# Layer 1 of a four-layer image network: narrower projection products, and the adding-up of the scan directions moved from VectorE to GpSimd

## The chip, the core and the metric

The kernel is one launch on one core of a Trainium2 chip. A core has five engines that run side by side, each with its own instruction queue that is worked off strictly in order: TensorE (PE, matrix products into the memory called PSUM), VectorE (DVE), ScalarE (ACT), GpSimd (POOL) and SyncE (SP, which here issues DMA transfers). Operands lie in SBUF (128 partitions) or in PSUM. The metric is the device time of the launch in microseconds, the median over several runs.

## The reference: what is computed

The input is 16 images of 96 channels and 56 x 56 pixels (L = 3136 pixels), in fp32. Layer 0 is a convolution block, layers 2 and 3 are spectral mixers with an 8-bit feed-forward part. The change is in layer 1 alone, a state-space block that scans each image in four directions (along the rows, along the columns, and both backwards):

```python
u = _ln(z, norm1_g, norm1_b) @ in_proj_w.T              # 96 -> 192 channels (Din)
uc = silu(depthwise_conv3x3(u))
xf = uc.reshape(B, Din, L)                               # pixels row by row
xt = jnp.transpose(uc, (0, 1, 3, 2)).reshape(B, Din, L)  # column by column
xs = jnp.stack([xf, xt, xf[..., ::-1], xt[..., ::-1]], axis=1)   # K = 4 directions
dbl = jnp.einsum('bkdl,kcd->bkcl', xs, x_proj_w)         # 8 rows for each direction
dts, Bs, Cs = jnp.split(dbl, [R, R + N], axis=2)         # R = 6, N = 1
dt = softplus(jnp.einsum('bkrl,kdr->bkdl', dts, dt_projs_w) + dt_projs_b[...])
a = jnp.exp(dt * A)
bb = dt * Bs * xs
# h[t] = a[t] * h[t-1] + bb[t], along L
y = h * Cs + Ds * xs
ym = sum of the four directions, each turned back to row order
z = z + _ln(ym, out_norm_g, out_norm_b) @ out_proj_w.T
z = z + gelu(_ln(z, norm2_g, norm2_b) @ fc1_w.T + fc1_b) @ fc2_w.T + fc2_b
return x + z
```

## The kernel before, in words

`kernel` (L1819) runs `layer0`, `layer1` and `layers23` one after the other. A second, general branch with `soft=True` is in the program too; it is entered only if a flag says so.

**Layer 1 (`layer1`, L839)** treats the 16 images one by one in four lanes that overlap: `fronts`, `makes`, `scans` and `backs` (L1398 to L1420). While one image is scanned, the front of a later image and the back of an earlier one run beside it.

- `front` (L998): squares and sums for the norm (L1028 to L1037), a reciprocal root on GpSimd (L1046), the projection to 192 channels (L1066), the 3 x 3 convolution as nine products of 64 x 64 tiles, four such tiles side by side (L1106), SiLU (L1129). Then `inputs` (L1136) makes the array `proj` of 128 x 3136: one product of all 128 columns for the four directions, 32 partitions for each (8 rows used, the others zero), in two parts of the contraction (L1142, L1143). ScalarE copies the upper half straight (L1145) and the lower half turned, into column order (L1150). A row of ones in `proj` (the bias `kone`) carries `dt_projs_b`. Four DMAs (L1159) write the B and C rows to a DRAM tensor `bc`.
- `made_of` (L1166): an image has 6 units in `ORDER` (`TILES`: 128 channels of direction 0, 1, 2 or 3, or the last 64 channels of two directions together), each in two halves, and each half in two subs of 784 pixels: 24 subs. For each, TensorE makes `p_d` (two products of 128 x 128 by 392 columns, L1183), ScalarE takes exp (L1190), ln(1 + .) (L1192), and exp of that times A (L1199). SyncE loads the B and C rows of the sub, repeated on all partitions, into a tile `bc` (L1210, L1214).
- `scanned` (L1221), on VectorE: for each sub `dt = dt * u` (L1254), `dt = dt * B` (L1257), the scan in place in `a` (L1261, backwards L1263), `dt = a * C` (L1269); then, for the first tile of an image accumulator, `y = u * D + dt` (L1274), and for all the others `y = y + dt` (L1280). Tiles 1 and 4 (`flip`) are in column order, so their L1254 and L1280 read `u` and `y` with a stride of 56 elements. At the end of an image one operation adds the turned half of `ym` (L1286).
- `back` (L1290): seven groups of 448 pixels, in two lanes (L1387): squares, output projection (L1309 to L1313), norms with two small reciprocal roots on GpSimd (L1328, L1351), transposes (L1357), the MLP (L1366 to L1376), the last sum (L1378) and the store (L1380).

**Order of the work.** Nothing is ordered by hand. Each step is announced by `yield Op(engine, cost, lag, take, give, ...)`, and `in_order` (L228) plays through all lanes with these costs and issues at each point the step that can start first; among equal starts the rank of its lane decides (L1400, L1405, L1411, L1417; less is earlier). So the costs and ranks fix each engine's queue when the program is built. `take` and `give` are counts of buffers (`buffers`, L846): "ps" are the PSUM pairs of two banks, "dt" the tiles of a sub.

Of the kernel before, what the change touches and what calls it, by code (L numbers as in the profile page):

```python
# [18 lines left out]
L = S * S  # L19
# [40 lines left out]
def packed(x):  # L60
# [32 lines left out]
    xp = np.zeros((P, 2 * P), f)  # L93
    wdt = np.zeros((P, 6, P), f)
    o["k_one"] = np.zeros((P, 1), f)
    for to, k in enumerate((0, 2, 1, 3)):
        xp[32 * to : 32 * to + R + 2, :DIN] = w("x_proj_w")[k]
        o["k_one"][32 * to + R + 2] = 1.0
        for i, halves in enumerate(TILES):
            at = 0  # L100
            for of, n in halves:
                if of == k:
                    d = slice(0, P) if n == P else slice(P, DIN)
                    wdt[32 * to : 32 * to + R, i, at : at + n] = w("dt_projs_w")[k, d].T
                    wdt[32 * to + R + 2, i, at : at + n] = w("dt_projs_b")[k, d]
                at += n
    o["l1_xp0"], o["l1_xp1"], o["l1_dt"] = xp[:, :P].T, xp[:, P:].T, wdt
# [731 lines left out]
def layer1(ctx, tc, src, given, dst, flags=None, soft=False):  # L839
# [3 lines left out]
    pairs, dram = ph.pool("ps", 4, space=PSUM), ph.pool("d", 3, space=bass.MemoryType.DRAM)  # L843
# [3 lines left out]
        "ps": 4, "x": 1, "half": 1, "xc": 2, "big": 7, "proj": 1, "dt": 5, "a": 2, "bc": 2, "xn": 1,  # L847
        "ysq": 1, "o": 2, "z": 2, "zn": 1, "zt": 1, "hid": 1, "xr": 2,
# [9 lines left out]
    n1, n2, no, xp0, xp1, wdt, kone, ds, fc1b, fc2, fc2b = ph.loads(  # L858
        "l1_n1", "l1_n2", "l1_no", "l1_xp0", "l1_xp1", "l1_dt", "k_one", "l1_d", "l1_fc1b", "l1_fc2", "l1_fc2b"
# [22 lines left out]
    def bounded():  # L882

        size = lambda out, in_: nc.vector.scalar_tensor_tensor(out, in_, -1.0, in_, ALU.mult, ALU.max)
        w, wx, wt = staged([C, DIN]), [staged([P, P]) for _ in range(2)], staged([P, 6 * P])
        nc.vector.tensor_tensor(w, win, win, ALU.mult)
        for out, in_ in (*zip(wx, (xp0, xp1)), (wt, wdt.rearrange("p i n -> p (i n)"))):
            size(out, in_)
        u, c, s = (ph.c([P, 2], n) for n in ("bound_u", "bound_c", "bound_s"))
        p = pair("p_b")  # L890
        for i, n in enumerate((P, 64)):
            nc.tensor.matmul(p[:n, 0, i : i + 1], w[:, P * i : P * i + n], ones[:C, 0, 0:1], start=True, stop=True)
        nc.vector.memset(u, 0.0)
        for i, n in enumerate((P, 64)):
            nc.vector.tensor_scalar(u[:n, i : i + 1], p[:n, 0, i : i + 1], float(C * C), None, ALU.mult)
# [102 lines left out]
    def front(b, it):  # L998
# [159 lines left out]
        for g in range(4):  # L1158
            nc.sync.dma_start(bc[g], proj[32 * g + 6 : 32 * g + 8])  # L1159
# [694 lines left out]
```

## Time and profile before

| quantity | us |
|---|---|
| median of 3 runs | 7367.89 (7360.73 to 7368.41) |
| the profiled execution, its own time | 7355.87 |
| its span, first to last instruction | 7354.1 |
| layer 1: first L1028 to last L1380 starts | 1163.7 to 4662.2 |
| last operation of an image's scan, L1286: first start, last start | 1459.8, 4505.3 |
| from there, one image of 15: (4505.3 - 1459.8) / 15 | 203.0 |

In the profile, "busy" is the time in which an engine executes; DMA-issuing, register and semaphore instructions are not counted. An fp32 product shows as two MATMUL records. "L1280" is line 1280 of the kernel before. In a group's row, the shapes are partitions x elements, output before input, then the count, busy time, mean of one, and after a bar the idle time of the engine just before these instructions with what ended it.

### The profile page before, as it was taken

How to read it: one execution, taken by the hardware profiler on the slowest of the kernel's cores; microseconds unless marked ns; L12 is line 12 of the kernel's file. 1: busy time of each engine (PE TensorE's matmuls, PEld its weight loads, DVE VectorE, ACT ScalarE, POOL GpSimd, SP SyncE). 2: the span in 40 equal slices, each digit the busy share in tenths (PEclk: the TensorE clock that was granted, in tenths of full speed). 3: DMA queues.
4: the chain of work that ended last, by engine and by line, in shares of the span. 5: the costliest groups of instructions: out<-in, count | busy, mean ns of one | idle time of the engine just before them, and what ended most of it. 6: DMA issues, size and time to landing. Idle time of an engine off the chain costs nothing. (4 is left out here: it accounts for less than half of the span.)

```text
span 7354.1 us, 114424 instructions
## 1 busy us (share of the span) xinstructions
PE 6443.1 (88%) x46263; PEld 4671.9 (64%) x46263; DVE 5719.1 (78%) x7601; ACT 4640.5 (63%) x6129; POOL 1011.2 (14%) x738
## 2 busy tenths in 40 slices
PE   7999997788999889888989887688999999999986
PEld 4444444455656666555666655587888888888875
DVE  6887792888889988888888986367777778777775
ACT  4544453677777777777777773256666666666664
POOL 0000000011111111111111112111111111111110
PEclk9999998899999999999999988799999999999997
DMA  1111111444444444344434432354555554555542
GB/s 38 29 39 39 32 32 34 134 116 126 121 120 128 121 118 124 113 116 115 116 115 124 121 109 66 88 118 101 125 123 130 114 126 111 122 130 123 122 109 59
DMA packets 494411, 743.59 MB, mean 101 GB/s; under 512 B 200065, under 2 KB 329633, under 8 KB 490434
## 3 DMA queue, kind: packets, MB, share of 16 engines
q1 hardware_dynamic: 492754, 732.54, 38.5%
q8 instruction: 367, 6.01, 0.4%
q0 software_dynamic: 1120, 3.64, 0.2%
q14 instruction: 170, 1.39, 0.1%
HBM read 544.06 MB, written 191.99 MB: 100 GB/s over the span
## 5 line engine op out<-in xcount | busy, mean ns | idle before, releaser
L1554 POOL TENSOR_TENSOR r<-v,nhalf 112x16 f32<-112x16 f32 (+1 forms) x128 | 396.8, 3106 | 2238.3 <-DVE v L1552 1681.7
L1183 PE MATMUL p_d<-proj,l_dt 128*128 128x392 f32 x1536 | 627.3, 536 | 40.5 <-ACT proj L1150 13.2
L1254 DVE TENSOR_TENSOR dt<-dt,big 128x784 f32<-128x784 f32 x384 | 457.3, 1191 | 122.0 <-ACT a L1199 121.8
L779 DVE SCALAR_TENSOR_TENSOR h<-pad,rows,h 128x1568 f32<-128x1568 f32 x288 | 525.8, 1844 | 3.9
L1190 ACT ACTIVATE dt<-p_d 128x784 f32<-128x784 f32 x384 | 315.2, 821 | 261.8 <-PE p_d L1183 252.0
L1183 PEld LDWEIGHTS p_d<-proj,l_dt 128*128 128x128 f32 x1536 | 289.7, 204 | 250.2 <-issue 88.2
L1612 PE MATMUL p<-k_f,z 112*128 112x112 f32 x3072 | 376.1, 282 | 61.5 <-DMA z<-d 57.5
L1375 PE MATMUL p_g<-l_fc,hid 128*112 128x96 f32 x2688 | 384.9, 281 | 47.4 <-ACT hid L1369 42.1
L1612 PEld LDWEIGHTS p<-k_f,z 112*128 112x128 f32 x3072 | 371.3, 199 | 70.4 <-issue 55.1
L1660 PE MATMUL p_v<-w,gg 128*112 128x97 f32 x2048 | 376.4, 266 | 36.7 <-DVE gg L1649 11.6
L1375 PEld LDWEIGHTS p_g<-l_fc,hid 128*112 128x112 f32 x2688 | 337.6, 193 | 96.7 <-ACT hid L1369 72.7
L1106 PE MATMUL p_c<-x,taps 64*64 64x392 f32 x4608 | 393.7, 491 | 1.1 <-ACT hid L1369 1.1
L1127 ACT COPY big<-p_c 64x392 f32<-64x392 f32 (+1 forms) x448 | 267.5, 598 | 197.8 <-PE p_c L1106 192.8
L1199 ACT ACTIVATE a<-dt,aneg 128x784 f32<-128x784 f32 x384 | 345.3, 936 | 64.7 <-DVE a L1263 55.0
L1328 POOL TENSOR_TENSOR r<-v,nhalf 112x4 f32<-112x4 f32 x112 | 226.7, 2024 | 1144.2 <-DVE v L1326 1144.2
L1269 DVE TENSOR_TENSOR dt<-a,bc 128x784 f32<-128x784 f32 x384 | 373.5, 973 | 9.0
L1257 DVE TENSOR_TENSOR dt<-dt,bc 128x784 f32<-128x784 f32 x384 | 373.6, 973 | 8.7
L1661 PE MATMUL p_v<-w2both,gg 128*112 128x97 f32 x2048 | 374.3, 265 | 0.0
L1192 ACT ACTIVATE dt<-dt,one 128x784 f32<-128x784 f32 x384 | 363.9, 948 | 8.9
L1261 DVE TENSOR_TENSOR_SCAN a<-a,dt 128x784 f32<-128x784 f32 x192 | 352.3, 1835 | 5.6
L1263 DVE TENSOR_TENSOR_SCAN a<-a,dt 128x784 f32<-128x784 f32 x192 | 352.0, 1833 | 4.1
L1581 PE MATMUL p_a<-first,xt 97*112 97x192 f32 x1792 | 336.2, 335 | 17.1 <-ACT xt L1575 6.9
(341 smaller groups left out, 16502.6 us busy)
## 6 DMA issues: line engine op xcount, KB each, us to landing
bc<-bc SPq DMA_DIRECT2D x256, 784.0 KB
bc<-bc SPq DMA_DIRECT2D x256, 392.0 KB
d<-y SPq DMA_DIRECT2D x448, 192.0 KB
z<-d SPq DMA_DIRECT2D x128, 672.0 KB
d<-uu SPq DMA_DIRECT2D x256, 169.8 KB
z<-d SPq DMA_DIRECT2D x192, 194.0 KB
xc<-x SPq DMA_DIRECT2D x96, 336.0 KB
x<-in_x SPq DMA_DIRECT2D x16, 1176.0 KB
```

Of the source, the lines that this page charges most:

```text
L779: nc.vector.scalar_tensor_tensor(out, view, taps9[:, i : i + 1], out, ALU.mult, ALU.add)
L1106: nc.tensor.matmul(p[to : to + 64, b, :TC], taps[64 * s : 64 * s + 64, j, k], pad[64 * s : 64 * s + 64, r0 : r0 + 7, k % 3 : k % 3 + S], s ...
L1183: nc.tensor.matmul(p[:, b, :TC], wdt[:, i], proj[:, cols], start=True, stop=True)
L1192: nc.scalar.activation(dt, dt, AF.Ln, bias=one)
L1254: nc.vector.tensor_tensor(as_own(dt), as_own(dt), own(u), ALU.mult)
L1257: nc.vector.tensor_tensor(dt, dt, t[:, 0], ALU.mult)
L1269: nc.vector.tensor_tensor(dt, a, t[:, 1], ALU.mult)
L1375: nc.tensor.matmul(p[:Q, q, :C], hid[:, j, own], fc2[:, j], start=j == 0, stop=False)
L1554: nc.gpsimd.tensor_tensor(r, v, nhalf[:, :n], ALU.pow)
L1612: nc.tensor.matmul(p[:, q, :Q], flat[:, P * (3 * q + k) : P * (3 * q + k) + P], f2, start=True, stop=True)
L1660: nc.tensor.matmul(out, gs[2 * h][:, at + k], w["w2"][:, 2 * h], start=True, stop=False)
L1661: nc.tensor.matmul(out, gs[1][:, at + k], w["w2both"][:, h], start=False, stop=True)
```

## The change

1. **Products of 32 columns.** In place of `inputs`, three products of 32 stationary columns for each chunk of 392 pixels: one for directions 0 and 2, one whose moving operand is `u` read across (column order), one for the remaining 64 channels of both. Chunks 0 to 3 go to the four groups of 32 output partitions of one PSUM bank, chunks 4 to 7 to those of the next. `proj` shrinks to 128 x 2 x 392: its partition says the chunk and the row, and one ScalarE copy fills it. All four directions' rows lie together (24 rows of dt input, 8 rows of B and C).
2. **Products of 32 rows.** `p_d` contracts over the 32 partitions of its chunk; the two halves of a sub lie on different groups of 32 partitions and in different banks. The bias `dt_projs_b` is added by ScalarE's activation.
3. **`bc`** is ordered by chunk; the loads move the same bytes into the same tiles.
4. **The scan's input lies in PSUM.** `dt * B` is written to a fixed PSUM tile `driven` of two banks, and the scan reads it there; the pool of PSUM pairs has three instead of four.
5. **GpSimd adds `y = y + dt`.** The 16 additions of an image that are not the first of their accumulator leave VectorE's list; a new lane `sums` issues them on GpSimd after the multiplication by C. `dt` is given back only after that. L1286 waits for the last of them.
6. **Plan.** Ranks of the four lanes, the number of `dt` (5 to 4), `proj`, `xn`, `o`, `z`, `xr` buffers, and three lanes in `back` instead of two.

```diff
-    pairs, dram = ph.pool("ps", 4, space=PSUM), ph.pool("d", 3, space=bass.MemoryType.DRAM)
+    pairs, dram = ph.pool("ps", 3, space=PSUM), ph.pool("d", 3, space=bass.MemoryType.DRAM)
+    driven = ph.pool("drive", 1, space=PSUM).tile([P, 2 * 512], F32, tag="drive", name="drive")
...
-        "ps": 4, "x": 1, "half": 1, "xc": 2, "big": 7, "proj": 1, "dt": 5, "a": 2, "bc": 2, "xn": 1,
-        "ysq": 1, "o": 2, "z": 2, "zn": 1, "zt": 1, "hid": 1, "xr": 2,
+        "ps": 3, "x": 1, "half": 1, "xc": 2, "big": 7, "proj": 2, "dt": 4, "a": 2, "bc": 2, "xn": 2,
+        "ysq": 1, "o": 3, "z": 3, "zn": 1, "zt": 1, "hid": 1, "xr": 3,
...
-        it["proj"] = proj = buf([P, L], "proj")
...
-                nc.tensor.matmul(p[:, b, :T], xp0, us[0][:, cols], start=True, stop=False)
-                nc.tensor.matmul(p[:, b, :T], xp1, us[1][:, cols], start=False, stop=True)
...
+        it["proj"] = proj = buf([P, 2, TC], "proj")
+        chunk = lambda t, c: t[:, TC * c : TC * c + TC]
+        across = lambda t, c: turned(t)[:, 7 * c : 7 * c + 7]
+        for b in range(2):
+            yield pe(3, 0.7, ("ps",) if b == 0 else ())
+            p = pair("p_x") if b == 0 else p
+            for k in range(3):
+                for q in range(4):
+                    moving = (chunk(us[0], 4 * b + q), across(us[0], 4 * b + q), chunk(us[1], 4 * b + q))[k]
+                    nc.tensor.matmul(p[32 * q : 32 * q + 32, b, :TC], xw[:, k], moving, start=k == 0, stop=k == 2)
+        yield act(2 * TC, give=("ps",))
+        nc.scalar.copy(proj, p[:, :, :TC])
+        it["bc"] = bc = dram.tile([8, 2, 4, TC], F32, tag="bc", name="bc")
         yield Op("SP", 1.4, 4.0, post=it["ready"])
...
+        for q in range(4):
+            nc.sync.dma_start(bc[:, :, q], proj[32 * q + 4 * R : 32 * q + 32])
...
-                    yield pe(2, 0.66)
+                    yield pe(1, 0.75)
                     p = pair("p_d")
                     for b in range(2):
-                        cols = slice(HALF * h + SUB * s + TC * b, HALF * h + SUB * s + TC * b + TC)
-                        nc.tensor.matmul(p[:, b, :TC], wdt[:, i], proj[:, cols], start=True, stop=True)
+                        on = slice(32 * (2 * s + b), 32 * (2 * s + b) + 32)
+                        nc.tensor.matmul(p[:, b, :TC], wdt[on, i], proj[on, h], start=True, stop=True)
...
-                        nc.scalar.activation(flat, p[:, :, :TC], AF.Exp)
+                        nc.scalar.activation(flat, p[:, :, :TC], AF.Exp, bias=dtb[:, i : i + 1])
...
-                    nc.vector.tensor_tensor(dt, dt, t[:, 0], ALU.mult)
+                    b = driven[:, :SUB]
+                    nc.vector.tensor_tensor(b, dt, t[:, 0], ALU.mult)
...
-                        nc.vector.tensor_tensor_scan(a, a, dt, first, ALU.mult, ALU.add)
+                        nc.vector.tensor_tensor_scan(a, a, b, first, ALU.mult, ALU.add)
...
-                    yield dve(SUB, give=("bc",) + (("a",) if end else ()))
+                    yield dve(SUB, give=("bc",) + (("a",) if end else ()), post=None if i in (0, 2) else added[unit, s])
                     nc.vector.tensor_tensor(dt, a, t[:, 1], ALU.mult)
...
-                        yield dve(SUB, 1.85e-3 if flip else 1.04e-3, give=give + (("big",) if free else ()))
-                        nc.vector.tensor_tensor(own(y), own(y), as_own(dt), ALU.add)
...
+            yield Op("none", 0.0, 0.0, wait=it["summed"])
             yield dve(L, 1.85e-3)
             nc.vector.tensor_tensor(image(ym[:64]), image(ym[:64]), turned(ym[64:]), ALU.add)
 
-        yield from scan()
+        def sums():
+            for unit in units:
+                i, h = unit
+                back = i >= 3
+                if i in (0, 2):
+                    continue
+                for s in ((1, 0) if back else (0, 1)):
+                    at = HALF * h + SUB * s
+                    yield Op("none", 0.0, 0.0, wait=added[unit, s])
+                    y, u = it["y"][i == 5], (um if i == 5 else u0)
+                    dt = made[unit][s]
+                    if i in (1, 4):
+                        out = turned(y)[:, at // S : at // S + 14]
+                        dt = dt.rearrange("p (w h) -> p w h", h=S)
+                    else:
+                        out = y[:, at : at + SUB]
+                    free = i in (4, 5) and unit == [k for k in units if k[0] == i][-1] and s == 0
+                    yield Op("POOL", 1.9, give=("dt",) + (("big",) if free else ()), post=it["summed"] if free and i == 5 else None)
+                    nc.gpsimd.tensor_tensor(out, out, dt, ALU.add)
+                    if free:
+                        big.append(u)
+
+        yield [scan(), sums()]
...
-        yield [some(range(0, NT, 2)), some(range(1, NT, 2))]
+        yield [some(range(k, NT, 3)) for k in range(3)]
...
-            yield 3 * b - 9
+            yield 3 * b + -3
             yield from front(b, items[b])
...
-            yield -1
+            yield -100
...
-            yield 99
+            yield -200
...
-            yield 3 * b
+            yield 3 * b + 3
```

## The prediction

> **What bounds the kernel now.** First the table by stages. The 13 images between 1663 and 4302 us each take 203.0 us, and the last back part runs alone from 4505 on (columns: start:end and length, then busy time and count of each engine, the granted clock, the DMA share, GB/s).
>
> ```profile
> core 0: us, PE busy (x) PEld busy (x) DVE busy (x) ACT busy (x) POOL busy (x), PEclk, DMA share, GB/s
> 1663.00:4302.00 2639.00, 2367.34 (x16488) 1579.00 (x16489) 2317.30 (x2693) 1967.85 (x2542) 450.62 (x378) 0.94 0.41 119
> 4505.00:4665.00 160.00, 116.58 (x761) 90.41 (x759) 45.92 (x115) 39.24 (x75) 33.17 (x35) 0.84 0.09 23
> ```
>
> Divided by 13, an image has PE 182.1 us busy, DVE 178.3, ACT 151.4, POOL 34.7. Two engines are near 90% of 203, and neither fills it: in fixed queues each waits some 20 to 25 us for the other. A change has to relieve both. Next, who makes DVE wait in that stretch (total, times, longest):
>
> ```profile
> DVE z L1378 <- PE p_g L1376: 108.1, 24, 9.9
> DVE dt L1254 <- ACT a L1199: 41.5, 42, 4.7
> DVE zn L1353 <- POOL r L1351: 36.6, 41, 1.2
> ```
>
> The largest wait is for PE (8.3 us an image). Then the groups by shape in the same stretch, which price what the change touches:
>
> ```profile
> L1183 PE MATMUL p_d<-proj,l_dt 128*128 128x392 f32 x1240 | 505.5, 534 | 18.4 <-ACT x L1070 12.4 <-ACT zt L1360 3.3 <-DVE z L1337 1.2
> L1254 DVE TENSOR_TENSOR dt<-dt,big 128x784 f32<-128x784 f32 x312 | 371.6, 1191 | 41.5 <-ACT a L1199 41.5
> L1106 PE MATMUL p_c<-x,taps 64*64 64x392 f32 x3744 | 320.3, 491 | 1.1 <-ACT hid L1369 1.1
> L1263 DVE TENSOR_TENSOR_SCAN a<-a,dt 128x784 f32<-128x784 f32 x156 | 285.9, 1833 | 3.1
> L1280 DVE TENSOR_TENSOR big<-big,dt 128x784 f32<-128x784 f32 x207 | 271.3, 1311 | 5.4
> L1106 PE MATMUL p_c<-half,taps 64*64 64x392 f32 x1872 | 160.1, 491 | 0.0
> L1142 PE MATMUL p_x<-big,l_xp 128*128 128x448 f32 x182 | 83.4, 539 | 0.0
> L1150 ACT ACTIVATE proj<-p_x,k_one 64x896 f32<-64x896 f32 x38 | 73.8, 1942 | 0.6
> ```
>
> Last, the question on which the result hangs: what do DVE and POOL do to each other? The timeline of two short POOL operations, each with the DVE operations beside it (start, duration):
>
> ```profile
> 2031.08 1.85 DVE L1261 TENSOR_TENSOR_SCAN a<-a,dt 128x784 f32<-128x784 f32 x1
> 2032.96 0.97 DVE L1269 TENSOR_TENSOR dt<-a,bc 128x784 f32<-128x784 f32 x1
> 2031.31 2.42 POOL L1328 TENSOR_TENSOR r<-v,nhalf 112x4 f32<-112x4 f32 x1 [11.98 <-DVE v L1326]
> ...
> 2885.24 0.17 DVE L1037 COPY me<-p_s 112x8 f32<-112x8 f32 x1 [0.63 <-PE p_s L1035]
> 2884.70 1.01 POOL L1328 TENSOR_TENSOR r<-v,nhalf 112x4 f32<-112x4 f32 x1 [15.94 <-DVE v L1326]
> ```
>
> Alone, the root takes 1.01 us. Beside a scan with two SBUF inputs it takes 2.42: it stands until the scan ends at 2032.93 and finishes 0.80 us later. It gets in at the 0.03 us between two DVE operations that depend on each other, before L1269.
>
> [...] The trace shows only the 64x64 case: L1106's 5616 records are 54 groups of four products per image, and (320.3 + 160.1) / 13 / 54 = 0.68 us for four, where one lone 128x128 product of L1183 takes 505.5 / 13 / 48 = 0.81 us.
>
> **Part by part, per image.**
>
> *L1280 leaves DVE:* 271.3 / 13 = 20.9 us, so 178.3 - 20.9 = 157.4. The product by B into PSUM and the scan from it: existing DVE rows with a PSUM operand (L1337, 548 ns) cost what those without do (L1335, 550 ns), so zero; bounds -0 and +0.05 us on 48 operations, 2.4 us.
>
> *Sixteen additions on POOL:* [...] 1.9 us[...]; 30 us in all. POOL's time is free (34.7 + 30 of 203). Half of them write and read `y` in column order; on DVE that stride makes 0.97 us into 1.66 (L1254's view by line: 960 ns least, 970 median, 1683 most), so the bound above is 1.9 x 1.7 = 3.2 us for those[...].
>
> *What they do to DVE* is the unknown. An addition is released when L1269 ends. DVE's next operation is mostly the next sub's L1254, two SBUF inputs, already started when POOL arrives; POOL waits. L1257 depends on L1254, so there is a gap, and by the timeline above POOL gets in there. L1257 has two SBUF inputs too and stands until the addition is over; behind it stand the scan, L1269, and every front and back step on DVE. The scan from PSUM[...] comes afterwards. Bounds: 0 (all adds fall under scans) and 16 x 1.9 = 30 us, more with the stride. I take 25: some adds meet one-input operations (L1337, L1344, L1346, L1378, together 15 us an image) or a DVE that waits anyway, at L1286 for one. DVE is then occupied for 157.4 + 25 = 182 us, slightly more than before.
>
> *PE:* four records of a sub's `p_d` take 1.48 us in the timeline; two products side by side (1.48 - 0.17) / 2 + 0.17 = 0.83, so 24 x 0.83 = 19.9 in place of 38.9. `p_x`: (83.4 + 83.2) / 13 = 12.8 become six groups of four, 6 x 0.83 = 5.0; if the reads across are twice as slow, 6.4; if columns don't run side by side, 16. PE falls to 155 (up to 166).
>
> *ACT:* the two copies into `proj`, (39.0 + 8.0 + 73.8 + 12.8) / 13 = 10.3, become one of 0.8: 142. [...]
>
> *SP and DMA:* as many loads of the same bytes; DVE never waits for `bc` in this stretch, so zero; the cover is the second tile, 8 us long. The four stores of B and C shrink in rows, zero.
>
> *Buffers:* three PSUM pairs for four, four `dt` for five, and `dt` held 2 to 4 us longer by POOL. These give waits back: more lanes against fewer pairs. Roots on POOL can stand behind an addition, 1.9 us, 14 times, in three lanes.
>
> *Sum.* DVE's idle 24.7 us shrinks, as PE, its main releaser, has 27 us less; the scans now also rank first. I put 11 us (bounds 8 and 17). 182 + 11 = 193 per image, 10 less than 203; over 15 images -150. The last back part: seven groups in two lanes are four rounds of 40 us in 160; in three lanes three rounds, 120, but PE alone needs 117, so 135: -25. The first front, with its `p_x` and copies on the only path: -8. Together -183 from the profiled execution's 7355.9 (span 7354.1 and 1.8 around it): 7173. The shown median, 7367.9, lies 12 above; on its scale 7185, and I say 7180.
>
> **Rivals.** *(A) The additions ride under the scans for nothing.* For it: 1.9 us of adding against 1.83 us of scan, and a PSUM operand was chosen; POOL may be refused at the gap. Against it: roots do get in at such gaps. DVE 160, PE 155: idle as now, 17; 177 per image: 15 x -26 - 33 = -423, so 6945. *(B) Slower: each addition holds DVE longer than the 1.31 us it saves, by too much.* DVE stands for t per addition: 157.4 + 16 t - 5 hidden + 13 idle = 205 is break-even with the 33 us of tail and front counted, so t = 2.5 us. With 3.2 us for the strided half the mean is 2.5; with contention on both, or a slower addition, 2.8: 210 per image, 15 x 7 - 33 = +72, so 7440. *(C) The narrow products don't run side by side*, as the trace shows only 64x64: PE stays at 182 + 3, DVE at 182, both bounds remain: 202 per image, 7330.
>
> **How the numbers follow.** Forecast case 0.50 (idle 8 to 17 and hold 20 to 30 us: 7080 to 7300), A 0.22 (6890 to 7060), C 0.06, B 0.22, of which 0.03 ends within 0.2%. 0.2% is 15 us, about what a measurement of this kernel tells from no change. Faster 0.77, same 0.03, slower 0.20. The likeliest case's own range is 7080 to 7300; the range for 8 in 10 takes in most of A and the near part of B: 6920 to 7420.
>
> **What would show it.** Right: POOL additions of about 1.9 us alone and near 3 when they wait; L1257's successor with idle time or a duration near 2.7 us behind such an addition; DVE's busy time near 157 or, if the stand is counted as busy, 182; PE near 155, `p_d` halved; ACT 142. A would show additions starting or stretching into scans with DVE's L1257 at 0.97 us and no gap. B would show them at 2.5 us or more with DVE standing as long. Wrong altogether: DVE idle for ACT's `a` or for PSUM pairs by more than 20 us an image, which would put the bound in the buffers.

## The result, and the profile after

| | before | after |
|---|---|---|
| median of 4 runs each, us | 7365.27 (7360.73 to 7368.41) | 7282.26 (7275.73 to 7297.03) |
| ratio, 95% interval | | 0.9891 (0.9873 to 0.9908) |
| the profiled execution / its span | 7355.87 / 7354.1 | 7277.09 / 7275.2 |
| granted TensorE clock, mean over the span | 0.934 | 0.906 |
| last operation of a scan (L1286; after: L1270), first start | 1459.75 | 1450.04 |
| the same, last start | 4505.26 | 4475.40 |
| from there to the last store of layer 1 | 157.0 | 109.0 |

The change gains 83 us, 1.1%. The forecast was 7180, a gain of some 185: the direction and the range hold, the size does not. The rows split the profiled gain of 78.8 us: the first image -9.7 (forecast -8), the 15 scans -20.1 (forecast -150), the tail -48.0 (forecast -25). So the missing gain is in the scans, which fall short by 130 us; the tail gave 23 us more than was forecast and makes up for a part of it.

The stages of after, ten images in steady state and the tail (columns as in the table by stages of before):

```profile
core 0: us, PE busy (x) PEld busy (x) DVE busy (x) ACT busy (x) POOL busy (x), PEclk, DMA share, GB/s
2066.40:4079.80 2013.40, 1772.14 (x13154) 1129.74 (x13153) 1835.93 (x1954) 1472.17 (x1926) 787.98 (x462) 0.89 0.42 121
4475.50:4584.50 109.00, 96.11 (x705) 78.93 (x703) 40.16 (x101) 34.48 (x67) 21.34 (x25) 0.94 0.10 26
```

Divide the first line by ten: a period of 201.3 us, DVE 183.6 busy, PE 177.2, ACT 147.2, POOL 78.8. The forecast had 193, 182, 155 and 142. DVE is as occupied as was said; its idle time is 17.7 us where 11 was put, and PE is busy for hardly less than before's 182.1. ACT's 147.2 holds 2.2 us that the forecast did not count: the exp that carries the bias takes 0.915 us in the median (L1180 of after), the exp without it 0.823 (L1190 of before), 24 times an image. The clock in this stretch is 0.89, where before had 0.94. The second line is the tail: PE is busy for 96 us of it and not for the 117 of before, at a clock of 0.94 and not 0.84.

What VectorE waits for in the same ten images (total, times, longest):

```profile
DVE dt L1243 <- ACT a L1189: 55.6, 42, 2.1
DVE z L1384 <- PE p_g L1382: 49.5, 32, 2.9
DVE me L1037 <- PE p_s L1035: 12.5, 27, 0.8
DVE zn L1359 <- POOL r L1357: 12.3, 10, 1.5
DVE v L1331 <- ACT o L1323: 5.7, 10, 1.5
DVE xn L1061 <- PE p_r L1056: 5.2, 11, 0.8
```

Beside the three waits that the prediction shows, before has these in its 13 images:

```profile
DVE me L1037 <- PE p_s L1035: 33.5, 38, 1.7
DVE v L1325 <- ACT o L1317: 32.3, 15, 2.9
DVE xn L1061 <- PE p_r L1056: 9.2, 7, 3.1
```

The 8.3 us an image for `p_g` have become 5.0, and the wait for ACT's `a` has grown from 3.2 to 5.6. All the waits of DVE that the profile puts down to PE add up to 11.7 us an image before and to 6.8 after, those for ACT to 5.8 and 6.3. The long waits for `p_g` have gone (longest 2.9 us, before 9.9). The groups by shape of the same ten images:

```profile
L1290 POOL TENSOR_TENSOR big<-big,dt 128x784 f32<-128x784 f32 x160 | 431.8, 2699 | 564.8 <-DVE dt L1259 414.2 <-PE p_f L1372 54.7 <-DMA x<-z 41.5
L1247 DVE TENSOR_TENSOR drive<-dt,bc 128x784 f32<-128x784 f32 x240 | 394.1, 1642 | 5.1
L1243 DVE TENSOR_TENSOR dt<-dt,big 128x784 f32<-128x784 f32 x240 | 307.2, 1280 | 58.2 <-ACT a L1189 55.6 <-POOL big L1290 2.4
L1173 PE MATMUL p_d<-proj,l_dt 32*128 32x392 f32 x960 | 245.9, 590 | 116.9 <-DVE z L1343 49.0 <-DVE z L1384 44.2 <-ACT hid L1375 11.1
L1253 DVE TENSOR_TENSOR_SCAN a<-a,drive 128x784 f32<-128x784 f32 x120 | 219.5, 1829 | 2.9
L1143 PE MATMUL p_x<-big,l_xw 128*32 128x392 f32 x480 | 69.1, 723 | 0.0
```

The counterpart of L1247 in before's 13 images, and all additions of after (count, then shortest, median and longest in ns):

```profile
L1257 DVE TENSOR_TENSOR dt<-dt,bc 128x784 f32<-128x784 f32 x311 | 302.6, 973 | 6.9
L1290 POOL TENSOR_TENSOR big<-big,dt x256: 1837/2451/4027, 1319.0 to 4473.3; 128x784 f32<-128x784 f32 x128
```

An addition takes 2.70 us on POOL in the mean of the ten images. Of the 256, the 128 that write `y` in column order take 2.23 us at the least, the other 128 take 1.84. The product by B (L1247) takes 1.64 us in the mean, where L1257 took 0.97: it has no new idle time in front of it, so its standing still is counted as busy. The scan from PSUM, 1.83 us, costs what it cost from SBUF.

How this happens shows in the timeline around one addition (start, duration):

```profile
2545.89 0.97 DVE L1259 TENSOR_TENSOR dt<-a,bc 128x784 f32<-128x784 f32 x1
2546.78 1.63 DVE L1243 TENSOR_TENSOR dt<-dt,big 128x784 f32<-128x784 f32 x1
2548.45 2.90 DVE L1247 TENSOR_TENSOR drive<-dt,bc 128x784 f32<-128x784 f32 x1
2551.38 1.85 DVE L1253 TENSOR_TENSOR_SCAN a<-a,drive 128x784 f32<-128x784 f32 x1
...
2547.03 3.48 POOL L1290 TENSOR_TENSOR big<-big,dt 128x784 f32<-128x784 f32 x1 [3.84 <-DVE dt L1259]
```

The addition is issued at 2547.03, stands behind L1243, which ends at 2548.41, gets in at the gap of 0.04 us, and ends at 2550.51. L1247 begins at 2548.45, ends at 2551.35, 0.84 us after the addition, and so lasts 2.90 us in place of 0.97. That is the picture that the prediction drew from the small operations on POOL (the reciprocal roots).

### The profile page after: what moved, and what is told of

It reads as the page before. It is cut to its first block, busy times and chain, and to the rows that moved or that the text cites. A ratio compares the mean times of both kernels' runs of the same rounds, so it can differ in the third digit from the quotient of the medians.

```text
span 7275.2 us, 115240 instructions
## 1 busy us (share of the span) xinstructions
PE 6324.3 (87%) x46587; PEld 4522.3 (62%) x46587; DVE 5752.0 (79%) x7344; ACT 4529.8 (62%) x6019; POOL 1682.2 (23%) x994
## 5 line engine op out<-in xcount | busy, mean ns | idle before, releaser
L1290 POOL TENSOR_TENSOR big<-big,dt 128x784 f32<-128x784 f32 x256 | 691.0, 2699 | 957.4 <-DVE dt L1259 756.8
L1247 DVE TENSOR_TENSOR drive<-dt,bc 128x784 f32<-128x784 f32 x384 | 627.5, 1634 | 12.8 <-DMA bc<-bc 4.5
L1243 DVE TENSOR_TENSOR dt<-dt,big 128x784 f32<-128x784 f32 x384 | 489.7, 1275 | 162.4 <-ACT a L1189 159.6
L1173 PE MATMUL p_d<-proj,l_dt 32*128 32x392 f32 x1536 | 404.9, 613 | 171.4 <-DVE z L1343 58.8
L1180 ACT ACTIVATE dt<-p_d,l_dtb 128x784 f32<-128x784 f32 x384 | 350.9, 914 | 275.1 <-PE p_d L1173 226.4
L1381 PE MATMUL p_g<-l_fc,hid 128*112 128x96 f32 x2688 | 393.3, 289 | 24.8 <-ACT hid L1375 10.8
L1253 DVE TENSOR_TENSOR_SCAN a<-a,drive 128x784 f32<-128x784 f32 x192 | 351.3, 1830 | 4.8
L1251 DVE TENSOR_TENSOR_SCAN a<-a,drive 128x784 f32<-128x784 f32 x192 | 351.1, 1829 | 4.1
L750 PE MATMUL p_c<-pad,taps 64*64 64x392 f32 x4032 | 347.3, 493 | 0.3 <-ACT pad L732 0.3
## 6 DMA issues: line engine op xcount, KB each, us to landing
d<-y SPq DMA_DIRECT2D x448, 192.0 KB
```

The source lines that it names most:

```text
L1173: nc.tensor.matmul(p[:, b, :TC], wdt[on, i], proj[on, h], start=True, stop=True)
L1243: nc.vector.tensor_tensor(as_own(dt), as_own(dt), own(u), ALU.mult)
L1247: nc.vector.tensor_tensor(b, dt, t[:, 0], ALU.mult)
L1290: nc.gpsimd.tensor_tensor(out, out, dt, ALU.add)
L1381: nc.tensor.matmul(p[:Q, q, :C], hid[:, j, own], fc2[:, j], start=j == 0, stop=False)
```

## The experiments

**The theories.** The forecast theory: a POOL addition holds DVE for about 1.56 us (25 us for 16), and the rest is DVE's idle time, which TensorE's lighter work shrinks. Once the result was known, three explanations stood for the idle time that did not shrink: the buffers (three PSUM pairs, four `dt`), the order in which the plan lays out the steps, and the lower clock. A rival to all: the additions cost much more than they hold DVE for.

"Same order" below means that every engine's queue has the order of the kernel named; "anew" that costs or buffers in the plan changed, so that the order was laid out anew. The image is the mean of nine images in steady state, busy times are per image with overlaps counted once, both from each run's own profile. (Before's first five images are shorter, so its 206.2 here stands beside 203.0 over all fifteen.) The ratio is to runs of the kernel before made beside it (medians 7351 to 7365).

| run | order | median us | ratio to before (95%) | image | PE | DVE | clock |
|---|---|---|---|---|---|---|---|
| before | | 7365 | 1 | 206.2 | 184.9 | 180.2 | 0.95 |
| after | | 7282 | 0.9891 (0.9873 to 0.9908) | 201.4 | 177.6 | 183.5 | 0.89 |
| no_adds | after's | 7059 | 0.9607 (0.9590 to 0.9624) | 185.8 | 169.7 | 158.9 | 0.94 |
| adds_dve_same | after's | 7178 | 0.9757 (0.9740 to 0.9773) | 195.3 | 174.4 | 177.5 | 0.91 |
| pd_twice | after's | 7413 | 1.0082 (1.0065 to 1.0099) | 210.0 | 191.9 | 182.2 | 0.91 |
| adds_dve | anew | 7343 | 0.9986 (0.9977 to 0.9995) | 209.0 | 176.0 | 178.5 | 0.88 |
| late_c | anew | 7297 | 0.9926 (0.9908 to 0.9944) | 205.3 | 181.1 | 168.0 | 0.89 |
| narrow_only | anew | 7177 | 0.9764 (0.9746 to 0.9782) | 191.1 | 171.9 | 178.2 | 0.94 |
| n_jitter | anew | 7308 | 0.9937 (0.9917 to 0.9956) | 197.5 | 173.4 | 178.5 | 0.91 |
| n_pairs3 | anew | 7651 | 1.0399 (1.0381 to 1.0416) | 228.9 | 191.2 | 180.7 | 0.84 |
| n_ranks | anew | 7481 | 1.0176 (1.0159 to 1.0193) | 216.5 | 185.3 | 178.5 | 0.86 |
| n_lanes3 | anew | 7457 | 1.0138 (1.0121 to 1.0155) | 215.7 | 181.4 | 180.0 | 0.85 |
| after_pairs4 | anew | 7429 | 1.0103 (1.0087 to 1.0120) | 219.8 | 189.6 | 179.3 | 0.86 |
| narrow_same | before's | 7463 | 1.0147 (1.0130 to 1.0164) | 212.8 | 182.0 | 180.1 | 0.86 |
| same_wide1 | before's | 7476 | 1.0171 (1.0154 to 1.0188) | 214.4 | 192.0 | 180.6 | 0.91 |
| same_narrow2 | before's | 7569 | 1.0296 (1.0279 to 1.0313) | 219.9 | 198.5 | 180.6 | 0.88 |
| same_wide2 | before's | 7551 | 1.0272 (1.0255 to 1.0289) | 220.6 | 202.8 | 180.6 | 0.95 |

**1. no_adds: after without the additions.**

```diff
-                    nc.gpsimd.tensor_tensor(out, out, dt, ALU.add)
```

> The changed kernel with its 16 GpSimd additions an image left out (12 of 24 subs of two accumulators then lack their sum; the plan and every queue stay as they are). Theory 'hold': the additions cost VectorE 26 us an image (39.4 + 30.7 - 23.3 - 28.6 and the small operations that stood, about 24 us by the groups), so VectorE falls from 183.6 to about 159 us and the image from 201.5 to 180 to 185: 7282 - 15 x 19 = about 7000 us. Rival 'PE and plan': TensorE, its lower clock and the fixed order with three PSUM pairs bound the image at 201; then the time stays within 7230 to 7290 us although VectorE's busy time falls.

Measured: 7059, an image of 185.8 us. The nine images of after and of no_adds, and the product by B in no_adds:

```profile
2267.50:4079.70 1812.20, 1598.26 (x11863) 1017.73 (x11863) 1651.06 (x1755) 1322.19 (x1729) 714.66 (x414) 0.89 0.42 121
2222.70:3895.20 1672.50, 1527.14 (x11864) 998.72 (x11862) 1429.75 (x1755) 1316.67 (x1729) 321.16 (x270) 0.94 0.45 131
L1247 DVE TENSOR_TENSOR drive<-dt,bc 128x784 f32<-128x784 f32 x216 | 211.8, 981 | 4.6
```

The durations of DVE's operations add up to 167.4 us an image here and to 192.2 in after, in the same order: the 16 additions hold DVE for 24.8 us, 1.55 each; 16.0 of it is the product by B, 2.1 the product by `u`, and the rest small operations of the front and the back. The period differs by 15.6 us only, since 26.9 us of idle (185.8 - 158.9) have become 17.9: a third of the hold falls where DVE waited anyway. The idle time matters as much: with no additions at all, DVE has 27 us to wait. The forecast's rival A had put 177 for this case.

**2. adds_dve_same: the additions on VectorE, in after's order.**

```diff
-                    nc.gpsimd.tensor_tensor(out, out, dt, ALU.add)
+                    nc.vector.tensor_tensor(out, out, dt, ALU.add)
```

> The changed kernel with its own plan to the letter: each of the 16 additions an image is issued at the same place of the order, but on VectorE instead of GpSimd. Theory 'hold': VectorE gets 20.9 us an image of additions (1.31 us each) in place of 24.8 us of standing, so the image is about as long as the changed kernel's or 2 to 3 us shorter: 7230 to 7285 us. If moving them to GpSimd did relieve VectorE: longer than 7320 us.

```profile
2239.40:3997.40 1758.00, 1569.90 (x11864) 1009.97 (x11864) 1597.77 (x1899) 1321.47 (x1729) 334.76 (x270) 0.91 0.43 125
```

7178, 104 us less than after, 195.3 us an image against 201.4. The only difference is the engine of the addition. On DVE the 16 take 20.9 us, on POOL they hold DVE for 24.8. With overlaps counted once, DVE is busy for 177.5 us and in after for 183.5, and its idle time is alike, 17.8 and 17.9: so the 6.1 us an image that the move costs are DVE's own busy time. Part 5 of the change, taken by itself in this order, is a loss, and what gains lies in the other parts.

**3. narrow_only and adds_dve: the parts separately, order laid out anew.** narrow_only is before with parts 1 to 3 alone (and two `proj` tiles). adds_dve is after with the additions issued on VectorE by the plan, right behind the product by C.

```diff
-                    yield pe(2, 0.66)
+                    yield pe(1, 0.75)
-                        cols = slice(HALF * h + SUB * s + TC * b, HALF * h + SUB * s + TC * b + TC)
-                        nc.tensor.matmul(p[:, b, :TC], wdt[:, i], proj[:, cols], start=True, stop=True)
+                        on = slice(32 * (2 * s + b), 32 * (2 * s + b) + 32)
+                        nc.tensor.matmul(p[:, b, :TC], wdt[on, i], proj[on, h], start=True, stop=True)
```

> The kernel before with the narrow products alone (32-column and 32-row products, bias in the activation, new order of bc); scan from SBUF, four pairs, five dt, additions on VectorE, ranks and two lanes as before. Theory 'PE term': TensorE's work falls by some 20 us an image by the groups' rows, VectorE's stays at 178; the image goes from 203 to about 195, the time to about 7250 us. Rival 'clock': [...] the granted clock falls from 0.95 towards 0.89 and gives most of TensorE's saving back, the image stays at 200 to 203, 7320 to 7365 us.

> The changed kernel with the 16 additions back on VectorE (narrow products, scan from PSUM, three pairs, four dt, ranks and three lanes kept; the plan is laid out anew). Theory 'hold': an addition on GpSimd costs VectorE as much (about 24 us an image) as the addition itself did (20.9 us), so the time is the same or a little better than the changed kernel's: 7220 to 7290 us. Rival 'GpSimd relieves VectorE': the image gets about 10 to 20 us longer, 7400 us and more.

narrow_only gives 7177 and an image of 191.1 us, without the additions on POOL, the PSUM scan, the third lane or the new ranks:

```profile
2266.80:3986.80 1720.00, 1546.85 (x11872) 1001.92 (x11873) 1603.81 (x1899) 1314.14 (x1730) 327.23 (x270) 0.94 0.44 128
```

adds_dve, which has the same work per engine as adds_dve_same, gives 7343, more than was expected, where that gave 7178. The order alone is worth 165 us here, twice the change's whole gain.

**4. late_c: the hold taken away from L1247.** The product by C is issued later, between the next sub's product by `u` and its product by B, so that the addition which it releases meets other operations.

```diff
+                    if late is not None:
+                        yield from late
                     yield dve(SUB, wait=bct[unit, s])
...
-                    nc.vector.tensor_tensor(dt, a, t[:, 1], ALU.mult)
+                    late = times_c(unit, s, end, dt, a, t, own(y), own(u), mixed)
```

> The changed kernel with one reordering: VectorE's multiplication by C of a sub is issued after the next sub's product by u and just ahead of its product by B, so that the GpSimd addition is released while the product by B already runs, and gets in at the gap ahead of the scan, which reads one operand from PSUM. Theory 'hold': the additions now lie under the scans, VectorE's product by B falls from 1.64 to 0.97 us, its busy time from 183.6 to 160 to 165 us an image, and the time to about 7000 to 7080 us. Rival 'PE and plan': VectorE's busy time falls but the image stays near 200 us, 7250 to 7300 us.

The hold does fall: the product by B goes from 39.5 to 27.6 us an image, all of DVE's durations from 192.2 to 179.2. The time does not: 7297, 205.3 us an image with 37 us of idle. That is the time that the rival had put, but not by its cause alone: DVE has less work and longer waits, and the order was laid out anew. So the run doesn't price the hold; it shows that less work for DVE is no shorter time by itself.

**5. n_pairs3, n_ranks, n_lanes3, after_pairs4: the plan's parts one by one.** The first three put one part of after's plan each into narrow_only: three pairs; the ranks of the four lanes (one line of them is shown); three lanes in the back part, with a third buffer each of `o`, `z` and `xr`. The last takes the PSUM scan out of after and gives the fourth pair back.

```diff
-    pairs, dram = ph.pool("ps", 4, space=PSUM), ph.pool("d", 3, space=bass.MemoryType.DRAM)
+    pairs, dram = ph.pool("ps", 3, space=PSUM), ph.pool("d", 3, space=bass.MemoryType.DRAM)
```
```diff
-            yield 3 * b - 9
+            yield 3 * b + -3
```
```diff
-        yield [some(range(0, NT, 2)), some(range(1, NT, 2))]
+        yield [some(range(k, NT, 3)) for k in range(3)]
```
```diff
-                    b = driven[:, :SUB]
+                    b = dt
```

> The narrow products alone (7177 us) with three PSUM pairs for four, everything else equal. Theory 'pairs': the pair taken for the scan's input is what costs the changed kernel most of the 18 us an image by which its plan lies above this one (209 against 191 with the additions on VectorE): about 205 us an image, 7370 us. Rival 'ranks and lanes': three pairs cost little, 7180 to 7220 us.

> The narrow products alone (7177 us) with the changed kernel's ranks (scans -200, makes -100, fronts 3b - 3, backs 3b + 3), four pairs, two lanes. Theory 'pairs': little changes, 7150 to 7210 us. Rival 'ranks and lanes': with scans and makes first the fronts and backs come late, and the image is 200 us or more, 7310 us.

> The narrow products alone (7177 us) with three lanes in the back part and o, z and xr three times. By the changed kernel's last part (109 and 87 us where the narrow products alone have 116 and the kernel before 157) it gains 10 to 30 us there; in the middle nothing by theory 'pairs' (7145 to 7175 us), or a loss of several us an image by 'ranks and lanes' (7230 us and more), since three groups at once hold more pairs.

> The changed kernel with the product by B and the scan back in SBUF, so four pairs; additions stay on GpSimd. Theory 'hold': the additions get in ahead of the product by B in any case, so the scan from PSUM kept nothing free and VectorE's busy time stays at 183 us. If the pairs cost the image most of its idle time it falls from 201 to 190 to 195 us: 7110 to 7190 us. If the scan from PSUM was worth something (some additions lie under scans), VectorE's busy time rises above 190 and the time stays at 7280 us or above.

Each single edit makes narrow_only slower, by 474, 304 and 280 us; after has all three and more and lies 105 above it. A fourth pair given back to after, with the scan's input back in SBUF, makes it 147 us slower. Each of these runs has a new order as well, and the effects do not add up, so none of them can be read as the price of a buffer; that three pairs are the bound is not shown, and not excluded either. n_lanes3 shows one effect that stays: its tail is 87 us where narrow_only's is 116, for seven groups in both, so three lanes shorten the tail.

**6. n_jitter: a number that does no work.** In narrow_only the plan's cost of the four stores of B and C is 1.5 in place of 1.4. No instruction is added or taken away.

```diff
-        yield Op("SP", 1.4, 4.0, post=it["ready"])
+        yield Op("SP", 1.5, 4.0, post=it["ready"])
```

> The narrow products alone (7177 us) with one number of the plan changed that does no work: the cost put down for the four small stores of B and C, 1.4 to 1.5 us. The order is laid out anew from it. If the plan's order is steady, the time stays at 7165 to 7190 us. If it is a lottery (three single edits of the plan each cost 280 us and more), it moves by more than 30 us, up more likely than down: 7230 us.

7308: 131 us slower, more than the change as a whole gains. The images are no longer alike: of the 15, eight take 186 to 192 us and seven 208 to 221. So the time of one laid-out order says little about the edit that led to it: here a difference of 131 us comes from the order alone.

**7. pd_twice: the price of TensorE's work.** Each pair of products for `dt` in after is done twice.

```diff
-                    for b in range(2):
+                    for b in (0, 1, 0, 1):
```

> The changed kernel with every 32-row product of p_d done twice into the same place (second pair overwrites the first with the same values): 24 x 0.86 = 20 us an image more TensorE work, nothing else. If TensorE is no longer a bound in the changed kernel (the prediction: VectorE alone), the time stays within 7280 to 7330 us. If TensorE still sets much of the image's length (the order waits for it), it grows by half of that or more: 7430 us and above.

One undisturbed pair in after, and two in a row in pd_twice, each with the first product behind it:

```profile
2277.02 0.93 PE L1173 MATMUL p_d<-proj,l_dt 32*128 32x392 f32 x4
2277.88 0.43 PE L1034 MATMUL p_s<-ones,xc 96*112 96x96 f32 x2
...
2402.91 1.58 PE L1173 MATMUL p_d<-proj,l_dt 32*128 32x392 f32 x8
2404.43 2.52 PE L1066 MATMUL p_in<-xn,w_in 96*128 96x448 f32 x6
```

From first start to the next group's start a pair takes 0.86 us and two take 1.52 (the medians too, where no gap follows), so the second adds 0.66: 15.8 us an image, not the 20.6 expected. TensorE's busy time grows by 14.3 us, as the clock is 0.91 in place of 0.89, and the image takes 8.6 us more. The total lies between the two marks of the expectation. In this order a microsecond of added TensorE work is worth between 0.5 (8.6 / 15.8) and 0.6 (8.6 / 14.3) of one, with what the clock did counted in.

**8. narrow_same: before's order to the letter, with the narrow products.** All 24 products for B, C and the dt rows are issued where before issued the first of its four groups; the places of the other three are left empty.

```diff
-            for b in range(banks):
-                cols = slice(896 * g + T * b, 896 * g + T * b + T)
-                nc.tensor.matmul(p[:, b, :T], xp0, us[0][:, cols], start=True, stop=False)
-                nc.tensor.matmul(p[:, b, :T], xp1, us[1][:, cols], start=False, stop=True)
+            if not got:
+                got.append(g)
+                for b in range(2):
+                    for k in range(3):
+                        for q in range(4):
...
+                            nc.tensor.matmul(
+                                p[32 * q : 32 * q + 32, b, :TC], xw[:, k], moving, start=k == 0, stop=k == 2
+                            )
```

> The kernel before with the narrow products put into its own plan to the letter: the plan's costs, counts and order are those of before, and the three other p_x steps and the turned copies do nothing. So the order is not laid out anew. TensorE's load falls by 15 us an image (slots of 0.86 for 1.32 us, 24 times, and 6 for 10.5), VectorE's stays at 178. If the narrow products themselves bring the gain of the narrow-only kernel (177 us), 7150 to 7220 us. If most of that came from the new order, 7280 to 7340 us.

TensorE has less to do, nothing else has more, no order is changed but that of the 24 products, and it is 107 us slower than before, at a clock of 0.86. (TensorE's busy time, 182.0 us for 184.9, hardly shows the relief: at the lower clock the same products take longer, those of `p_o` 27.3 us an image in place of 24.0. In before's nine images a record of `p_s` takes 0.262 us in the median where the granted clock is full and 0.394 where it is half.) Whether the clock is the cause was then open, and three more runs asked it.

**9. same_narrow2, same_wide1, same_wide2: work given back to TensorE in narrow_same.** The pair twice; or ahead of the pair one, or two, products of before's form whose result is written over.

```diff
+                    for b in range(1):
+                        nc.tensor.matmul(p[:, b, :TC], wdt[:, i], proj[:, h], start=True, stop=True)
```

> The kernel before with the narrow products, in before's own order to the letter, and each pair of products for dt done twice: the second time with the same operands into the same places, so that the result is unchanged and TensorE has 24 x 0.86 = 20.6 us an image more to do, which is about what before had. Without the second pair the image took 209.8 us at a granted clock of 0.86, against 203.0 at 0.95 before. Theory G [...]: with the work back the clock comes back to 0.93 or more and an image takes 203 to 207 us; layer 1 is as slow as before or faster than the run with single products. Theory R [...]: the clock stays at 0.86 or under and the image takes 209.8 + some 8 = 218 us, total near 7590. Theory O (the clock has nothing to do with it, the moments at which products end have): the clock may be anything, the image is near 218 too.

> The same kernel with single narrow products, but ahead of each pair one product of 128 rows, 128 columns and 392 pixels into the first of the two banks, whose result is thrown away (the narrow product writes over it): some 24 x 0.66 = 16 us an image more for TensorE, in the form that before used. Theory G: as with the narrow pair done twice, clock 0.92 to 0.95, image 203 to 207 us. Theory R: here, and not with the narrow pair twice, the clock comes back to 0.93 or more, image 203 to 207, total 7350 to 7420. Theory O: image about 209.8 + 7 = 217, total near 7570.

> As the run before, with two such products, one into each bank: exactly before's products for dt, and after them the narrow pair. TensorE has before's work and 24 x 0.86 = 20.6 us an image on top. Theory R: clock 0.95 or more, image 203 plus what the extra narrow pair costs, 203 to 211. Theory G: the same. Theory O: image over 220.

Nine images of before, of narrow_same, and of the runs with one and with two wide products (all in before's order):

```profile
2244.00:4100.30 1856.30, 1663.72 (x11658) 1115.71 (x11656) 1621.55 (x1899) 1382.18 (x1790) 319.08 (x268) 0.95 0.41 118
```
```profile
2280.70:4195.50 1914.80, 1637.70 (x11826) 1067.19 (x11826) 1620.74 (x1898) 1318.85 (x1727) 312.39 (x268) 0.86 0.39 115
```
```profile
2278.10:4207.40 1929.30, 1728.11 (x12258) 1069.63 (x12260) 1625.81 (x1899) 1320.72 (x1727) 312.71 (x269) 0.91 0.39 114
```
```profile
2297.60:4282.90 1985.30, 1825.16 (x12691) 1126.91 (x12690) 1625.79 (x1899) 1320.31 (x1726) 304.14 (x268) 0.95 0.38 111
```

With one wide product the clock rises from 0.86 to 0.91, TensorE is busy for 10 us more, and the period stays: in both runs the images from the eighth to the fourteenth take 215 us each. With two, the clock is before's 0.95 and the image takes 220.6. The time did not come back with the clock, so what G and R put for the time is missed; O, which put all near 218, is the nearest. But the clock came back only together with added work, so these runs don't price the clock by itself. In the traces the granted clock is either full or half, in stretches of whole steps of 3.41 us (the last of a trace apart): 266 stretches in before, 294 in after. An image of 215.0 us is 63 such steps, and one of 221.9 us, to which both runs with two extra products settle, is 65. Of the 63, narrow_same has 18 at half clock and the run with one wide product 11: by estimate (7 x 3.41 / 2) 12 us of TensorE's time given back, which the added products took up and more. On the clock alone R, which put 0.86 or under for the narrow pair done twice and 0.93 or more with one wide product, is half right: TensorE busy for 90% of the time has 0.88 with the first and 0.91 with the second.

Where narrow_same loses its time shows in DVE's waits in the nine images, before and narrow_same:

```profile
DVE v L1325 <- ACT o L1317: 26.9, 10, 2.9
DVE me L1037 <- PE p_s L1035: 24.5, 25, 1.7
```
```profile
DVE v L1326 <- ACT o L1318: 59.0, 25, 3.6
DVE me L1036 <- PE p_s L1034: 47.6, 27, 4.3
```

These two grow by 32.1 + 23.1 = 55.2 us, 6.1 an image, and the image grew by 6.5. They are steps of the front and the back, whose inputs come from ACT and PE. `p_d` itself, which was made faster, is in neither. The products behind them, `p_s` and `p_o`, do meet the lower clock: 31% and 18% of their records begin in a step at half clock, before 12% and none. With one wide product these shares fall to 13% and 2%; the wait of `v` then falls to 38.3 us, but that of `me` stays, at 51.8. So the lower clock is a candidate for a part of these waits, and no run isolates it.

## Why the prediction was right in its direction and wrong in its size

**The step that failed** is the sentence in *Sum*: "DVE's idle 24.7 us shrinks, as PE, its main releaser, has 27 us less; the scans now also rank first. I put 11 us (bounds 8 and 17)." Measured: 17.9 us. Occupied 183.5 and idle 17.9 are 201.4; 182 and 11 were the forecast's 193. Of the 8.4 us too little, 6.9 are this idle time. Over the whole scan stretch the miss is 130 us: 34 in the first of the 15, which takes 226.7 us, and on average 6.9 in each of the other 14. The first one does not come from the additions: it takes 219 us in no_adds and 221 in narrow_only, but 197 in before and 198 in adds_dve. It was in no term of the forecast.

Two things went into that sentence, and both were off.

*TensorE did not lose 27 us.* In no_adds, whose clock is about before's (0.94 to 0.95), it falls from 184.9 to 169.7: 15.2. The forecast took away the old pair at the mean busy time of its records, 1.62 us (38.9 / 24). That mean takes in the pairs that ran slowly, and 0.16 us by which a pair's last record overlaps the group behind it. It put in the new one at 0.83, worked out from an undisturbed pair. The old pair, undisturbed:

```profile
2283.57 1.48 PE L1183 MATMUL p_d<-proj,l_dt 128*128 128x392 f32 x4
2284.89 0.35 PE L1034 MATMUL p_s<-ones,xc 96*112 96x96 f32 x2
```

On one scale, first start to the next group's first start with no gap between, the old pair takes 1.32 us at the least and 1.35 in the median, and the new one 0.86: the new price was right, and the old one was too high. The `p_x` products were put at 12.8, the sum of two lines whose records overlap; counted once they are 10.7, and they fell to 6.9, where 5.0 was forecast. In after TensorE then shows 177.6; 7.9 us more than in no_adds for the same products, at 0.89 in place of 0.94. At pd_twice's 0.6 of busy time this would be some 5 us of the period, an estimate that no run isolates. As to the waiting of other engines, the same rate makes 15.2 us of relief worth about 9, not 14, an estimate too.

*Less of the idle time ended with PE than was to go.* The forecast let 14 us of idle go as PE got lighter, but all of DVE's waits that the profile puts down to PE are 11.7 us in before; in after 6.8 are left, and the waits for ACT have hardly changed. And the idle time goes with the order and the clock, not with one releaser: narrow_same took work from TensorE and kept the order, and DVE waited longer, elsewhere; narrow_only has 12.9 us of idle, and n_jitter, with the same work in another order, 19.0. no_adds, with 25 us less for DVE, waits 27. The sign that the prediction named for "wrong altogether", over 20 us of idle for `a` or PSUM pairs, did not appear in after (5.6 for `a`).

**What was right.** *The hold*: 25 us forecast, 24.8 measured, by the mechanism named; the net effect in the same order, 15.6, is near the 16 between the forecast's 193 and rival A's 177, each of which was too low by some 8.5 us. For operations with two SBUF inputs the traces now show both orders: the addition stands behind L1243 (3.48 us in the timeline above, where the shortest takes 1.84), and L1247 behind the addition (147 times in after, 2.89 us in the median, without one 0.98). Operations with one SBUF input did run beside an addition at their usual length, as the prediction took for granted: L1343, 0.548 us in the median of 26 that met one and of 86 that did not; L1352, 0.547 in 29 and in 83. Whether a scan from PSUM runs beside one is not shown: none of after's 384 scans met an addition. *The length of an addition*: 1.9 us was put ahead of the run, and no trace of before has such an addition; the shortest in after's trace is 1.84, and the mean 2.70 with its waits. Column order costs POOL 0.39 us (2.23 for 1.84), so the bound of 3.2 was not reached. *Scan from PSUM*: zero, 1.83 us before and after. *First image*: -9.7 for -8. *Tail*: -48 for -25; three lanes were right, and the size was off for two reasons. The forecast counted seven groups in the last 160 us, but ten end there, three of them of the image before:

```profile
L1380 SPq DMA_DIRECT2D x<-z x10: 317/318/318, 4529.3 to 4662.2; - x10
L1386 SPq DMA_DIRECT2D x<-z x10: 305/317/321, 4481.9 to 4584.4; - x10
```

Ten take 157 us in before's two lanes and 109 in after's three; seven take 116 and 87 (narrow_only, n_lanes3). And TensorE's 117 us there, the forecast's floor, were measured at a clock of 0.84; at 0.94 it is busy for 96.

**The rivals.** A falls by the hold. C falls, though its 202 us an image lie nearest to the measured 201: that is luck, since its cause is absent. The pair takes 0.86 us, two products side by side: in after's trace their records start in twos, 0.007 us apart, and those of `p_x` in fours. B's mechanism is there, since an addition holds DVE for 1.55 us and saves 1.31, and adds_dve_same shows the move to be a loss of 104 us; the 2.5 us of hold that it needed to end slower than before are not reached.

**What stays open.** Why the products in before's own order lengthen the waits of the front and the back: the lower clock and the 24 products in one block in place of four groups are candidates, and neither was tried by itself. Whether three pairs and four `dt` cost something in after's order. And how much of after's distance from 193 is this order, and how much any order would have: adds_dve against adds_dve_same (165 us) and n_jitter (131 us) give the size of the spread, not its best end. Two versions beat both kernels, narrow_only and adds_dve_same, at 7177 and 7178; both do the additions on VectorE. Neither time is a best one, since another order could lie above or below it.

## What to carry to other kernels

Moving an elementwise operation from VectorE to GpSimd did not pay here, because it held VectorE for longer (1.55 us) than the operation had taken there (1.31). Before such a move, look at what VectorE runs in the 2 us after the release, and count the hold, not GpSimd's free time. Where a program lays out the queues from costs, test a single edit with every queue's order kept (the same operation on another engine, done twice, or left out), since a number that does no work moved this kernel by more than the change did. Don't count work taken off an engine in full: doing some of it twice shows at what rate the period follows (0.5 to 0.6 here), and the old and the new price have to be taken on the same scale, from start to next start. Before counting on a shorter idle time, add up the waits that end with the engine made lighter: here they were 11.7 us an image where 14 were to go.

## What the runs showed of the hardware that was not expected

- A VectorE operation with two SBUF inputs which starts beside a GpSimd addition that already has its turn ends 0.84 us after it (2551.35 against 2550.51; 0.83 to 0.84 in all 147 cases of L1247 in after), about its own 0.97 us: it does hardly any of its work before, in this case.
- A GpSimd addition that reads and writes one operand with a stride of 56 elements takes 2.23 us at the least, one without 1.84. On VectorE the product with such a stride (L1254 before) takes 1.63 us in the median and without it 0.97.
- VectorE operations that read little stand too: `v` from `s` (112 x 4) took 2.88 us for seven in after and 1.07 in no_adds.
- The granted clock is full or half, in whole steps of 3.41 us, and a pipeline can settle on a whole number of them: 63 an image in narrow_same and with one wide product more, 65 in the two runs with two products more. Why it does is not shown.
- Equal shares of busy time don't give equal clocks: 0.88 with 90% in the form with narrow pairs done twice, 0.91 with 90% where one of the products is wide, in the same order. The amount of TensorE's work alone doesn't explain this pair of runs, and what else does, no run isolates.
